# Layer 1 of a four-layer graph network: the last unit's norm, sides and scores in steps beside the first five jobs, with row 2 of the pairs among them, and the second head's values two pairs later

## The chip, the cores and the metric

The kernel is one program on one core of a Trainium2 chip. The metric is the device time of an execution in microseconds (us). The engines are named as in the profile: PE (matrix products and transposes, with weight loads as PEld), DVE (elementwise work and reductions), ACT (activation functions, copies), POOL (small elementwise work, some DMAs), SP (DMA issue). PE's clock can be lowered by a throttle; the profile shows the granted share.

## What is computed

Four layers on N = 4096 nodes of width D = 64 with one dense 0/1 adjacency matrix, each of the form x = x + layer(relu(layernorm(x))). Layer 0 is attention with eight heads and an output attention. Layer 1, around which the change lies, is a hyperbolic attention over all pairs of nodes:

```python
def _L1_gnn_ref(x, adj, r, w_att, b_att):
    c = 1.0 / r[0] ** 2
    x_t = logmap0(x, c)                       # x * artanh(sqrt(c)|x|) / (sqrt(c)|x|)
    left = x_t @ w_att[:D, 0]
    right = x_t @ w_att[D:, 0]
    adj_att = sigmoid(left[:, None] + right[None, :] + b_att[0]) * adj
    x_local = logmap(x[:, None, :], x[None, :, :], c)     # for every pair of nodes
    support_t = einsum('ij,ijd->id', adj_att, x_local)
    return proj(expmap(x, support_t, c), c)

h = maximum(layernorm(x), 0)
x = x + _L1_gnn_ref(h, adj, ...)
```

Layers 2 and 3 are a mean over neighbours with a dense layer, and a weighted sum over at most 100 neighbours.

## The kernel before

The nodes lie as NB = 32 blocks of P = 128, in NG = 8 groups of G = 512 (GB = 4 blocks each). The stages run one after the other: preparation, layer 0's heads, its output attention, a transition, layer 1's pairs, layer 1's nodes, layers 2 and 3.

**Layer 0's heads** run as 16 units (two halves of the targets, eight heads). A unit goes through the blocks in pairs j0 = 0, 2, 4 and so on; `split_edges` (L1229) makes the signs `st`, then B and C, and PE sums products with them (L1599). Beside the pairs of a unit the next head's values are prepared by a generator, `coming`, advanced by the condition at L1725: in the first unit two steps a pair from j0 = NB/2 + 4 = 20 on. Among these steps is an addition to FT (L1303) that waits for a DMA.

**Layer 0's output attention** runs as four units u of OB = 8 blocks (L2225 to L2329). A unit's results are finished (`finish_unit`, L2174: small folds on PE, DVE arithmetic, a tanh on ACT at L2217, the addition to x at L2222) beside the first products of the unit after it; then `layer1_nodes` (L1906) runs beside that unit: the norm of the new x (`norm_steps`, L994), h, its squared length a, the scale xs and its 16-bit pieces in the tile `aug`, the logarithms la and lb, and the sums with w_att (left, nrb). `layer1_sides` (L1994) transposes the pieces of `aug` into the four "sides" XC, LC, XH, LH that the products of pairs read, one PE transposition of eight blocks and one copy for each; `layer1_scores` (L2004) splits `left` into three 16-bit parts, transposes them and stores and reloads them by DMA as MOV.

**The transition** is what is left for the last unit, blocks 24 to 31 (L2331 to L2373). Its `finish_unit` runs with twelve side copies of the first three units spread through it; then come the rest of these, the last unit's `layer1_nodes` step by step, its four sides and its scores, and only then the pairs begin. A table load for the square root (L2355) comes before, one for the logarithm inside (L1931), one for the sigmoid after (L1948).

**The pairs** (`pairs_fast`, L2412) are 36 jobs (gi, gj) of two groups. The list `rows` sets their order: (0,0), (1,1), then rows 7, 6, 5, 4, 3, 2, each as (gi,0) to (gi,gi), at last (1,0). The loop runs over n = -2 to 36 and in each n over four slots s. In a slot the jobs are at different depths: for job n + 2 (`later`) `distance` (two products pu, L2480 and L2481, and an activation, L2482) and `square`; for job n + 1 (`soon`) `score_pair` (products pl, L2460 and L2466, sigmoid, L2471), `factor` and `weigh` on DVE; for job n (`now`) `turn` (transposes and a DVE product), `sums` and `last_column` (products accj and acci, L2526); for job n - 1 `bring`, which adds accj to VT on DVE (L2572, L2574). `check_edges` puts checks of the adjacency's rows (L972, one DVE pass of 1024 each) beside. A pair of different groups needs scores in both directions; one of a group with itself needs one, and no `turn`.

When the last job of rows 6, 4 and 2 has been brought, the two groups above it (a quarter of the nodes) are complete, and their `nodes` chain (`finish_steps`, L2644, then norm and two pieces of h, `hs` at L3233) is appended to `ends`; `end_nodes` takes steps from it in the slots of the following jobs, one chain after the other. The quarter of groups 0 and 1 comes after the last job. `scales()` sets the constants of these chains, once, at n = 3. While jobs follow, a chain takes its roots from `inverse_root` (L980: a first guess on DVE, then twelve small operations on POOL), not from ACT.

Order: inside `in_order()` (L933) the instructions of PE, DVE and ACT keep the order in which they are written; this holds for the transition and for the pairs. SP and POOL are free, apart from their data. A waiting instruction holds up all that is written behind it on its engine.

Of the kernel before, what the change touches and what calls it, by code (L numbers as in the profile page):

```python
# [25 lines left out]
P = 128  # L26
# [815 lines left out]
def kernel(  # L842
# [235 lines left out]
    with ExitStack() as l0:  # L1078
# [405 lines left out]
        with ExitStack() as ha:  # L1484
# [52 lines left out]
            for hf in range(2):  # L1537
# [9 lines left out]
                for hd in range(NH):  # L1547
# [85 lines left out]
                    for j0 in range(0, NB, 2):  # L1633
# [91 lines left out]
                        if j0 >= (NB // 2 + 4 if first else NB // 2 - 4):  # L1725
                            with behind(*done_at):
                                for _ in range(2 if first else 1):
                                    next(coming, None)
# [178 lines left out]
        def layer1_nodes(bs, work, aug, last=False):  # L1907
# [3 lines left out]
            yield from norm_steps(bs, work, "fat")  # L1911
# [17 lines left out]
            nc.scalar.activation(zn, zn, AF.Sqrt)  # L1929
            if last:  # L1930
                nc.scalar.preload_act_table_set("natural_log")  # L1931
# [5 lines left out]
            xh = aug[:, bs, C_XH : C_XH + D]  # L1937
# [3 lines left out]
            nc.vector.tensor_scalar(zn, zn, sqc, None, ALU.mult)  # L1941
            nc.vector.reciprocal(zr, zn)
            nc.vector.tensor_scalar(zn, zn, CLIP, None, ALU.min)
            nc.scalar.activation(la, zn, AF.Ln, bias=one_t, scale=1.0)
            nc.scalar.copy(aug[:, bs, C_XH2 : C_XH2 + D], xh)
            last_log[:] = [nc.scalar.activation(lb, zn, AF.Ln, bias=one_t, scale=-1.0).ins]
            if last:
                nc.scalar.preload_act_table_set("sigmoid_and_others")  # L1948
            nc.vector.tensor_tensor(aug[:, bs, C_XL : C_XL + D], t, xh, ALU.subtract)
# [7 lines left out]
            for i in range(2):  # L1957
                c = C_EX + 4 * i
                nc.vector.tensor_copy(
                    aug[:, bs, c : c + 4].rearrange("p b (k e) -> p b k e", e=2),  # L1960
# [4 lines left out]
                    aug[:, bs, c : c + 4].rearrange("p b (k e) -> p b k e", e=2),  # L1965
# [5 lines left out]
            nc.vector.tensor_copy(aug[:, bs, C_XH3 : C_XH3 + D], xh)  # L1971
            nc.vector.scalar_tensor_tensor(pab, pib, -1.0, pib, ALU.mult, ALU.max)
            yield False
            for i, dst in enumerate((left, nrb)):
                t = fat("hw")
                nc.vector.tensor_tensor(
                    t, hb, wab[:, i : i + 1, :].to_broadcast([P, n, D]), ALU.mult
                )
                nc.vector.tensor_reduce(dst[:, bs], t, AX.X, ALU.add)
                yield False  # L1980
# [12 lines left out]
        def layer1_sides(bs, bank, aug):  # L1993
            for b0 in range(bs.start, bs.stop, OB):  # L1994
                sides = (XC, C_XL, P), (LC, C_XH, P), (XH, C_XH2, KA), (LH, C_XH3, KA)
                for dst, c, cols in sides:
                    pt = bank()
                    for b in range(OB):
                        nc.tensor.transpose(
                            pt[:cols, b * P : (b + 1) * P], aug[:, b0 + b, c : c + cols], ident16  # L2000
# [3 lines left out]
        def layer1_scores(bs, ps):  # L2004
# [12 lines left out]
            pt = ps.tile([3 * n, P], F32, name="ppt", tag="misc")  # L2017
# [12 lines left out]
        wlast = el.enter_context(tc.tile_pool(name="wlast", bufs=2, side="right"))  # L2030
        with ExitStack() as ob:
# [193 lines left out]
            for u in range(4):  # L2225
# [8 lines left out]
                for q in range(NQ):  # L2234
# [62 lines left out]
                    if q == 0 and pending:  # L2297
                        finish_unit(*pending)
                        beside = layer1_nodes(slice((u - 1) * OB, u * OB), work, aug)
# [5 lines left out]
                if u == 3:  # L2305
                    layer1_scores(slice(0, NB - OB), ps)
# [31 lines left out]
            def bring(copy):  # L2338
                copy(*asked.pop(0))

            with in_order():
# [13 lines left out]
                nc.scalar.preload_act_table_set("sqrt_and_others")  # L2355
                ask(3)
                bring(nc.scalar.copy)
                chain = layer1_nodes(slice(NB - OB, NB), wlast, aug, True)
                for copy in (None, None, 1, 0, 1, 0, 0, None):
                    next(chain)  # L2360
                    ask()
                    if copy is not None:
                        bring(nc.vector.tensor_copy if copy else nc.scalar.copy)
                rest = layer1_sides(slice(NB - OB, NB), side, aug)
                for copy in (nc.scalar.copy, nc.vector.tensor_copy) * 2:
                    ask()
                    while asked:
                        bring(nc.vector.tensor_copy)
                    copy(*next(rest))
                assert next(coming, None) is None  # L2370
                for _ in chain:
                    pass
                layer1_scores(slice(NB - OB, NB), ps)  # L2373
# [3 lines left out]
    nc.vector.tensor_scalar(pm, pc, MIN_NORM, None, ALU.max)  # L2377
# [34 lines left out]
    def pairs_fast(es, VT, nodes, scales):  # L2412
# [4 lines left out]
        nc.vector.tensor_scalar(rb, nrb, -1.0, None, ALU.mult)  # L2417
# [10 lines left out]
        rows = [[(0, 0)], [(1, 1)]]  # L2428
        rows += [[(gi, gj) for gj in range(gi + 1)] for gi in reversed(range(2, NG))]
# [6 lines left out]
        with ExitStack() as ss:  # L2436
# [130 lines left out]

            def bring(gi, gj):
# [6 lines left out]
                if (gi, gj) in final:  # L2575
# [5 lines left out]
                    if gi % 2 == 0 and gi:  # L2581
                        bank = lambda: ps_f.tile([P, G], F32, name="pf", tag="pf")
                        ends.append([nodes(gi * GB, bank, beside), 0])
# [22 lines left out]
            load_edges(*jobs[0])  # L2606
            with in_order():
                for n in range(-2, len(jobs) + 1):
# [3 lines left out]
                    if n == 3:  # L2612
                        scales()
                    for s in range(4):
# [577 lines left out]
    with ExitStack() as es:  # L3192
# [10 lines left out]
        def scales():  # L3203
# [4 lines left out]
            )  # L3208
            nc.vector.tensor_scalar(pabs, pabs, sqc, 2.0 * F_C, ALU.mult, ALU.mult)
# [93 lines left out]
```

## Time and profile before

| | us |
|---|---|
| median of 3 runs | 1894.47 |
| lowest and highest | 1887.88, 1898.22 |
| the profiled execution, its own time | 1883.13 |
| its span | 1881.4 |

The stages in that trace: heads until about 905, output attention to 1109, transition to 1134, pairs to about 1595, the nodes' tail to about 1626, layers 2 and 3 to the end. The order of some pairs in it, by the end of the job's addition to VT: (1,1) starts its addition at 1167.31, (7,0) at 1181.61, (3,3) at 1546.17, (2,0) at 1559.88, (2,1) at 1571.43, (2,2) at 1579.59 and (1,0) at 1593.04.

The page's table of slices gives PE's granted clock in tenths of full speed, 40 slices of 47 us; the groups' rows give an instruction's busy time, its mean in ns, and the idle time ahead of it with what ended it:

```profile
PEclk8899999999999999999899997999999999999999
...
L2482 ACT ACTIVATE yt<-pu,consts 128x512 f32<-128x512 f32 x144 | 98.5, 686 | 95.8 <-PE pu L2481 95.8
...
L2471 ACT ACTIVATE sg<-pl,rb 128x512 f32<-128x512 f32 x256 | 160.6, 677 | 9.8 <-PE pl L2466 7.1
```

Slice 24, from 1129 to 1176, has one of the lowest clocks after the start of the program. Over the pairs ACT's idle time lies nearly all ahead of L2482, ended by PE: PE is the later of the two there.

### The profile page before, as it was taken

Reading aid. Unit: us, or ns where it says so; the run is one execution under the profiler, and the core shown is the slowest. Engines: PE = TensorE matmul, PEld = TensorE weight load, DVE = VectorE, ACT = ScalarE, POOL = GpSimd, SP = SyncE. Lnnn points to the kernel's source line nnn. Section 1 sums busy time; section 2 is a strip of 40 time slices with the busy share of each in tenths; the row PEclk is TensorE's granted clock in tenths of the full one; section 3 lists DMA queues with packets and bytes.
Section 4 is the critical chain, followed back from the end, with each engine's and each line's share of the span. In section 5 each row is a group of like instructions: output and inputs, shape, how many; then the busy total and the mean of one; then the engine's idle time right before and its main releaser. Section 6 shows DMA issues by size and latency. Waiting matters only on the chain.

```text
span 1881.4 us, 43986 instructions
## 1 busy us (share of the span) xinstructions
PE 1730.8 (92%) x19023; PEld 810.1 (43%) x19023; DVE 1606.5 (85%) x2480; ACT 1421.4 (76%) x1469; POOL 119.8 (6%) x204
## 2 busy tenths in 40 slices
PE   5789988999989999999899988999999998899998
PEld 4344444444445445445444442333333333464333
DVE  5889999999989989999778887998899787666787
ACT  2859988899978988899589978777777775234565
POOL 2001100010000000000121100000011022000000
PEclk8899999999999999999899997999999999999999
DMA  8966555535411110110455524454533111874595
GB/s 112 173 152 101 106 74 85 129 131 193 168 52 53 52 50 27 52 41 2 136 191 184 182 96 152 163 185 155 181 118 114 60 40 49 281 205 142 176 342 177
DMA packets 145996, 239.06 MB, mean 127 GB/s; under 512 B 16676, under 2 KB 106100, under 8 KB 140256
## 3 DMA queue, kind: packets, MB, share of 16 engines
q1 hardware_dynamic: 131264, 194.02, 31.4%
q0 software_dynamic: 14528, 42.13, 12.9%
q8 instruction: 151, 2.47, 0.5%
q14 instruction: 53, 0.43, 0.1%
HBM read 245.37 MB, written 49.46 MB: 157 GB/s over the span
## 4 chain that ended last, share of the span: by engine, by line
PE 48%; DVE 26%; ACT 15%; issue 7%; DMA 3%; POOL 0%; SPq 0%; DVEq 0%; ACTq 0%; POOLq 0%
ACT st L1242 9%; DVE B L1248 9%; PE accj L2526 9%; PE acco L2272 4%; PE accC L1599 4%; DVE st L1236 3%; PE pv L3105 3%; PE sacc L3129 3%; PE pf L2516 3%; PE pl L2460 2%; DVE C L1256 2%; PE pu L2480 2%; PE pl L2466 2%; PE accB L1599 2%; ACT sqy L2492 1%
## 5 line engine op out<-in xcount | busy, mean ns | idle before, releaser
L1242 ACT ACTIVATE st<-srow,nt 128x2048 int8<-128x2048 f32 x352 | 682.1, 1994 | 84.9 <-DVE B L1248 84.2
L1248 DVE TENSOR_TENSOR B<-st,mres 128x1024 int32<-128x1024 int32 x256 | 311.0, 1219 | 26.1 <-ACT st L1242 17.3
L1599 PE MATMUL accB<-B,ybh 128*32 128x512 fp8e4 x3072 | 255.8, 381 | 20.3 <-DVE B L1248 20.1
L1599 PEld LDWEIGHTS <-ybh 128*32 128x32 bf16 (+1 forms) x6656 | 180.7, 97 | 210.9 <-issue 55.2
L1599 PE MATMUL accD<-B,ybh 128*32 128x512 fp8e4 x2048 | 207.6, 382 | 2.3 <-DVE h L1747 2.3
L1236 DVE TENSOR_SCALAR st<-srow,nt 128x2048 uint8<-128x2048 f32 x160 | 205.0, 1283 | 1.5
L2526 PE MATMUL accj<-sg,who 128*64 128x512 f32 (+1 forms) x512 | 195.6, 611 | 5.6 <-DVE sg L2519 5.5
L2526 PE MATMUL acci<-sg,who 128*64 128x512 f32 (+1 forms) x512 | 195.6, 611 | 0.0
L1599 PE MATMUL accC<-mres,ych 128*32 128x512 fp8e4 x1920 | 190.0, 379 | 0.0
L1599 PE MATMUL accC<-B,ycn 128*32 128x512 fp8e4 x1920 | 190.0, 379 | 0.0
L2482 ACT ACTIVATE yt<-pu,consts 128x512 f32<-128x512 f32 x144 | 98.5, 686 | 95.8 <-PE pu L2481 95.8
L1256 DVE TENSOR_TENSOR C<-B,mres 128x1024 int32<-128x1024 int32 x136 | 166.2, 1222 | 4.6 <-PE accC L1599 1.7
L2471 ACT ACTIVATE sg<-pl,rb 128x512 f32<-128x512 f32 x256 | 160.6, 677 | 9.8 <-PE pl L2466 7.1
L1599 PEld LDWEIGHTS <-ych 128*32 128x32 f16 x4096 | 116.3, 97 | 119.2 <-issue 15.8
L1599 PE MATMUL accL<-B,ybh 128*32 128x512 fp8e4 x1536 | 156.4, 382 | 4.9 <-DVE h L1746 4.9
L1599 PE MATMUL accC<-C,ych 128*32 128x512 fp8e4 x2176 | 145.9, 383 | 9.0 <-DVE C L1256 8.9
L972 DVE SCALAR_TENSOR_TENSOR raw<-raw 128x1024 f32<-128x1024 f32 x128 | 153.9, 1215 | 0.0
L1242 ACT ACTIVATE st<-srowo,nto 128x1024 int8<-128x1024 f32 x128 | 138.1, 1136 | 13.4 <-DVE B L1248 10.5
L3119 ACT ACTIVATE w3b<-pv 128x512 int16<-128x512 f32 x172 | 91.0, 597 | 55.7 <-ACT w3b L3119 23.2
L2460 PE MATMUL pl<-nm,noid 128*128 128x512 fp8e4 x256 | 82.0, 387 | 15.5 <-ACT sg L2471 15.3
L2500 DVE SCALAR_TENSOR_TENSOR yt<-sqy,yt 128x1024 f32<-128x1024 f32 x72 | 84.8, 1217 | 0.7 <-ACT sqy L2492 0.7
L2507 DVE SCALAR_TENSOR_TENSOR sg<-yt,sg 128x1024 f32<-128x1024 f32 x72 | 84.8, 1217 | 0.5 <-ACT sg L2471 0.5
(544 smaller groups left out, 2666.1 us busy)
## 6 DMA issues: line engine op xcount, KB each, us to landing
raw<-in_adj_dram SPq DMA_DIRECT2D x128, 512.0 KB, 4.4
mo<-edges SPq DMA_DIRECT2D x32, 512.0 KB, 3.9
noedge<-nmo POOLq DMA_DIRECT2D x32, 512.0 KB, 3.6
nm<-noedge SPq DMA_DIRECT2D x64, 256.0 KB, 3.0
m<-edges SPq DMA_DIRECT2D x32, 512.0 KB, 5.8
srow<-srow_d SPq DMA_DIRECT2D x15, 1024.0 KB, 9.1
mres<-in_adj_dram POOLq DMA_DIRECT2D x8, 1024.0 KB, 36.1
edges<-in_adj_dram POOLq DMA_DIRECT2D x8, 1024.0 KB, 14.9
```

Source lines behind the costliest of these rows:

```text
L972: nc.vector.scalar_tensor_tensor(raw, raw, 0.0, raw, ALU.is_gt, ALU.not_equal, accum_out=bad[:, c : c + 1])
L1236: nc.vector.tensor_scalar(st[:, i, :].bitcast(U8), srow, negs[:, i : i + 1], EDGE, ALU.is_gt, ALU.mult)
L1242: nc.scalar.activation(st[:, i, :], srow, AF.Sign, bias=negs[:, i : i + 1], scale=-1.0)
L1248: nc.vector.tensor_tensor(B.bitcast(I32), st.bitcast(I32), edges.bitcast(I32), ALU.bitwise_and)
L1256: nc.vector.tensor_tensor(C.bitcast(I32), B.bitcast(I32), edges.bitcast(I32), ALU.bitwise_xor)
L1599: ins = nc.tensor.matmul(acc[k * O : (k + 1) * O, :], lhsT=values, rhs=moving(k), start=start, stop=stop,)
L2460: nc.tensor.matmul(pl, lhsT=noid, rhs=nm[:, b, :].bitcast(F8), start=True, stop=False)
L2471: nc.scalar.activation(sg[:, b0 + k, :], pl, AF.Sigmoid, bias=rb[:, j : j + 1], scale=1.0)
L2482: nc.scalar.activation(far[gi, gj][:, b, :], pu, AF.Sigmoid, bias=nb_t, scale=2.0 * DIST_K / (DIST_S * DIST_S),)
L2500: nc.vector.scalar_tensor_tensor(y, squares.pop((gi, gj, b0)), F_K1, y, ALU.add, ALU.mult)
L2526: nc.tensor.matmul(acc[r : r + n, :], lhsT=XQ[:, src, cols], rhs=w, start=start, stop=stop)
L3119: nc.scalar.activation(wk, pvs[i, k], AF.Relu)
```

## The change

- The last unit's work leaves the transition and becomes a generator, `last_unit`, of twenty steps: one is taken in each slot of the jobs n = -2 to 2. In n = -2 and -1 it does the norm, in n = 0 the scale and the pieces in `aug`, in n = 0 (last slot) to 1 the sides, in n = 1 the logarithms, then left, nrb and in n = 2 the scores. Its PSUM tiles come from the pool of `turn`.
- For this unit both roots are taken by `inverse_root`; the table of the logarithm is loaded for `logs()`, and the sigmoid's back, in n = 1. The pieces go to a tile of their own, `aug_last`. All four side copies are DVE's. `rb` (the bias of the sigmoid) is set in two parts, and `pm` in `scales()`.
- The seven side copies of the other units that are left after `finish_unit` go alternately to ACT and DVE.
- Row 2 comes right behind (1,1), not ahead of (1,0), so that five jobs, (0,0) to (2,2), go before row 7. The chains of quarters are appended after the last jobs of rows 6, 4 and 3 (row 2 before), and take two steps in each slot but the first of row 3's jobs (2, 1 and 2 before, in rows 3 and 2). In (1,0) they take up to four a slot, before and after.
- The four row checks of n = -1 go, those of the slots begin at n = 3.
- The second head's values start at pair j0 = 24, not 20.

```diff
-                        if j0 >= (NB // 2 + 4 if first else NB // 2 - 4):
+                        if j0 >= (NB - 8 if first else NB // 2 - 4):
...
-            yield from norm_steps(bs, work, "fat")
+            yield from norm_steps(bs, work, "fat", beside=(last,))
...
             nc.vector.tensor_scalar(zn, ab, MIN_NORM, None, ALU.max)
-            nc.scalar.activation(zn, zn, AF.Sqrt)
             if last:
-                nc.scalar.preload_act_table_set("natural_log")
+                root = inverse_root("zn_root", zn, work)
+                nc.gpsimd.tensor_tensor(zn, zn, root, ALU.mult)
+            else:
+                nc.scalar.activation(zn, zn, AF.Sqrt)
...
+            xh = aug[:, :, C_XH : C_XH + D]
             nc.scalar.copy(xh, t)
             yield False
 
-            nc.vector.tensor_scalar(zn, zn, sqc, None, ALU.mult)
-            nc.vector.reciprocal(zr, zn)
-            nc.vector.tensor_scalar(zn, zn, CLIP, None, ALU.min)
-            nc.scalar.activation(la, zn, AF.Ln, bias=one_t, scale=1.0)
-            nc.scalar.copy(aug[:, bs, C_XH2 : C_XH2 + D], xh)
-            last_log[:] = [nc.scalar.activation(lb, zn, AF.Ln, bias=one_t, scale=-1.0).ins]
-            if last:
-                nc.scalar.preload_act_table_set("sigmoid_and_others")
-            nc.vector.tensor_tensor(aug[:, bs, C_XL : C_XL + D], t, xh, ALU.subtract)
+            def logs():
+                nc.vector.tensor_scalar(zn, zn, sqc, None, ALU.mult)
+                nc.vector.reciprocal(zr, zn)
+                nc.vector.tensor_scalar(zn, zn, CLIP, None, ALU.min)
+                nc.scalar.activation(la, zn, AF.Ln, bias=one_t, scale=1.0)
+                last_log[:] = [nc.scalar.activation(lb, zn, AF.Ln, bias=one_t, scale=-1.0).ins]
+
+            if not last:
+                logs()
+            nc.scalar.copy(aug[:, :, C_XH2 : C_XH2 + D], xh)
+            nc.vector.tensor_tensor(aug[:, :, C_XL : C_XL + D], t, xh, ALU.subtract)
...
             yield False
+            if last:
+                logs()
+                yield True
             for i, dst in enumerate((left, nrb)):
...
                     pt = bank()
                     for b in range(OB):
                         nc.tensor.transpose(
-                            pt[:cols, b * P : (b + 1) * P], aug[:, b0 + b, c : c + cols], ident16
+                            pt[:cols, b * P : (b + 1) * P],
+                            aug[:, b0 - bs.start + b, c : c + cols],
+                            ident16,
                         )
...
-        def layer1_scores(bs, ps):
...
-            pt = ps.tile([3 * n, P], F32, name="ppt", tag="misc")
+            pt = bank()[0 : 3 * n, 0:P]
...
+        aug_last = wlast.tile([P, OB, C_EL + KX], F16, name="aug_last", tag="aug", bufs=1)
...
-                        beside = layer1_nodes(slice((u - 1) * OB, u * OB), work, aug)
+                        us1 = slice((u - 1) * OB, u * OB)
+                        beside = layer1_nodes(us1, work, aug[:, us1])
...
-                    layer1_scores(slice(0, NB - OB), ps)
+                    layer1_scores(
+                        slice(0, NB - OB), lambda: ps.tile([P, G], F32, name="ppt", tag="misc")
+                    )
...
                 finish_unit(*pending, beside_unit)
-                nc.scalar.preload_act_table_set("sqrt_and_others")
-                ask(3)
-                bring(nc.scalar.copy)
-                chain = layer1_nodes(slice(NB - OB, NB), wlast, aug, True)
-                for copy in (None, None, 1, 0, 1, 0, 0, None):
-                    next(chain)
-                    ask()
-                    if copy is not None:
-                        bring(nc.vector.tensor_copy if copy else nc.scalar.copy)
-                rest = layer1_sides(slice(NB - OB, NB), side, aug)
-                for copy in (nc.scalar.copy, nc.vector.tensor_copy) * 2:
-                    ask()
-                    while asked:
-                        bring(nc.vector.tensor_copy)
-                    copy(*next(rest))
-                assert next(coming, None) is None
-                for _ in chain:
-                    pass
-                layer1_scores(slice(NB - OB, NB), ps)
-
-
-
-    nc.vector.tensor_scalar(pm, pc, MIN_NORM, None, ALU.max)
+                for k in range(7):
+                    ask(2)
+                    bring(nc.vector.tensor_copy if k % 2 else nc.scalar.copy)
+                assert not asked and next(coming, None) is None
+
+        def last_unit(bank, rb):
+
+            bs = slice(NB - OB, NB)
+            chain = layer1_nodes(bs, wlast, aug_last, True)
+            for _ in range(10):
+                yield next(chain)
+            sides = layer1_sides(bs, lambda: bank().bitcast(F16), aug_last)
+            for side in sides:
+                yield True
+                nc.vector.tensor_copy(*side)
+            yield from chain
+            layer1_scores(bs, bank)
+            yield True
+            nc.vector.tensor_scalar(rb[:, bs], nrb[:, bs], -1.0, None, ALU.mult)
...
-        nc.vector.tensor_scalar(rb, nrb, -1.0, None, ALU.mult)
+        seen_b = slice(0, NB - OB)
+        nc.vector.tensor_scalar(rb[:, seen_b], nrb[:, seen_b], -1.0, None, ALU.mult)
...
-        rows = [[(0, 0)], [(1, 1)]]
-        rows += [[(gi, gj) for gj in range(gi + 1)] for gi in reversed(range(2, NG))]
+        rows = [[(0, 0)], [(1, 1)], [(2, gj) for gj in range(3)]]
+        rows += [[(gi, gj) for gj in range(gi + 1)] for gi in reversed(range(3, NG))]
         rows.append([(1, 0)])
...
+            def bank():
+                return ps_f.tile([P, G], F32, name="pf", tag="pf")
...
-                    if gi % 2 == 0 and gi:
-                        bank = lambda: ps_f.tile([P, G], F32, name="pf", tag="pf")
-                        ends.append([nodes(gi * GB, bank, beside), 0])
+                    if gi in (3, 4, 6):
+                        ends.append([nodes(gi // 2 * 2 * GB, bank, beside), 0])
...
+            unit = last_unit(bank, rb)
             with in_order():
...
                     if n == 3:
+                        assert next(unit, None) is None
                         scales()
...
                         if now:
-                            end_nodes(s, 4 if not soon else 1 + s % 2 * (now[0] < 4) if s else 0)
+                            end_nodes(s, 4 if not soon else 1 + (2 < n and now[0] < 4) if s else 0)
+                        next(unit, None)
                         if s == 1 and soon:
                             factor(*soon)
-                        if n > 1 and soon and s % 2 == 0:
+                        if n > 2 and soon and s % 2 == 0:
                             check_edges(1 if busy else 2 if s or now[0] == now[1] else 1)
                         if s == 3 and soon:
                             weigh(*soon)
-                            check_edges(4 if n < 0 else 0)
...
+            nc.vector.tensor_scalar(pm, pc, MIN_NORM, None, ALU.max)
```

More of the change, by code (lines that the diff above doesn't have):

```diff
@@ L1936, in layer1_nodes @@
             nc.vector.tensor_tensor(t, hb, over(ps2, D), ALU.mult)
-            xh = aug[:, bs, C_XH : C_XH + D]
+            xh = aug[:, :, C_XH : C_XH + D]
             nc.scalar.copy(xh, t)
             yield False
-            nc.vector.tensor_scalar(zn, zn, sqc, None, ALU.mult)
-            nc.vector.reciprocal(zr, zn)
-            nc.vector.tensor_scalar(zn, zn, CLIP, None, ALU.min)
-            nc.scalar.activation(la, zn, AF.Ln, bias=one_t, scale=1.0)
-            nc.scalar.copy(aug[:, bs, C_XH2 : C_XH2 + D], xh)
-            last_log[:] = [nc.scalar.activation(lb, zn, AF.Ln, bias=one_t, scale=-1.0).ins]
-            if last:
-                nc.scalar.preload_act_table_set("sigmoid_and_others")
-            nc.vector.tensor_tensor(aug[:, bs, C_XL : C_XL + D], t, xh, ALU.subtract)
+            def logs():
[8 more added lines that the diff above has]
+            nc.vector.tensor_tensor(aug[:, :, C_XL : C_XL + D], t, xh, ALU.subtract)
             ef = work.tile([P, 2, n], F32, name="ef", tag="ef", bufs=1)
@@ L1959, in layer1_nodes @@
                 nc.vector.tensor_copy(
-                    aug[:, bs, c : c + 4].rearrange("p b (k e) -> p b k e", e=2),
+                    aug[:, :, c : c + 4].rearrange("p b (k e) -> p b k e", e=2),
                     e16[:, :, i].unsqueeze(2).to_broadcast([P, n, 2, 2]),
@@ L1964, in layer1_nodes @@
                 nc.vector.tensor_scalar(
-                    aug[:, bs, c : c + 4].rearrange("p b (k e) -> p b k e", e=2),
+                    aug[:, :, c : c + 4].rearrange("p b (k e) -> p b k e", e=2),
                     e16[:, :, 1 - i].unsqueeze(3).to_broadcast([P, n, 2, 2]),
@@ L1970, in layer1_nodes @@
                 )
-            nc.vector.tensor_copy(aug[:, bs, C_XH3 : C_XH3 + D], xh)
+            nc.vector.tensor_copy(aug[:, :, C_XH3 : C_XH3 + D], xh)
             nc.vector.scalar_tensor_tensor(pab, pib, -1.0, pib, ALU.mult, ALU.max)
             yield False
+            if last:
+                logs()
+                yield True
             for i, dst in enumerate((left, nrb)):
@@ L1999, in layer1_sides, with layer1_scores @@
                         nc.tensor.transpose(
-                            pt[:cols, b * P : (b + 1) * P], aug[:, b0 + b, c : c + cols], ident16
+                            pt[:cols, b * P : (b + 1) * P],
+                            aug[:, b0 - bs.start + b, c : c + cols],
+                            ident16,
                         )
                     yield dst[:, b0 * P : (b0 + OB) * P], pt[:cols]
-        def layer1_scores(bs, ps):
+        def layer1_scores(bs, bank):
             n = bs.stop - bs.start
```

## The prediction

> **What bounds the kernel now.** I read the page's busy shares first, then the table of windows around the place that the change cuts open, then the timeline there and at the end of the pairs.
>
> ```profile
> PE 1730.8 (92%) x19023; PEld 810.1 (43%) x19023; DVE 1606.5 (85%) x2480; ACT 1421.4 (76%) x1469; POOL 119.8 (6%) x204
> ```
>
> PE is nearly full over the whole, so time can only be won where PE is not. Windows (width, then busy us of PE, PE's weight loads, DVE, ACT, POOL, each with its count; then PE's granted clock, DMA share, GB/s):
>
> ```profile
> 1115.00:1120.00 5.00, 4.61 (x67) 4.51 (x65) 3.34 (x9) 2.96 (x4) 0.00 (x0) 1.00 0.00 0
> 1120.00:1125.00 5.00, 0.61 (x8) 0.45 (x7) 4.29 (x8) 4.14 (x7) 0.00 (x0) 0.99 0.00 0
> 1125.00:1130.00 5.00, 0.81 (x8) 0.82 (x9) 4.29 (x21) 4.76 (x9) 0.00 (x0) 0.50 0.00 0
> 1130.00:1135.00 5.00, 4.22 (x31) 3.12 (x29) 3.01 (x7) 2.89 (x4) 0.59 (x3) 0.50 0.09 29
> 1135.00:1140.00 5.00, 4.67 (x12) 1.05 (x10) 4.22 (x14) 4.89 (x7) 0.00 (x0) 0.50 0.96 273
> ...
> 1150.00:1155.00 5.00, 5.00 (x18) 0.98 (x14) 4.31 (x4) 3.50 (x6) 0.00 (x0) 0.78 0.94 311
> 1155.00:1160.00 5.00, 4.21 (x23) 0.98 (x22) 3.61 (x5) 4.66 (x7) 0.00 (x0) 1.00 0.11 33
> ```
>
> From 1120 to 1130 PE works 1.4 us of 10, its clock halves, and it stays halved until about 1152. This hole is what the change attacks: the last unit's norm and sides stand alone there, DVE and ACT passing single operations to each other. The timeline names its edges (start, us, instruction, in brackets the idle time before it and its releaser):
>
> ```profile
> 1118.33 0.42 ACT L2217 ACTIVATE nmo<-nmo 128x256 f32<-128x256 f32 x1 [1.36 <-DVE nmo L2216]
> 1118.77 1.28 ACT L2355 ACT_TABLE_LOAD   x1
> ...
> 1129.19 3.60 PE L1999 MATMUL trd<-ident,aug 128*128 128x128 f16 x32 [7.46 <-DVE aug L1959]
> 1133.57 0.61 PE L2480 MATMUL pu<-XAf,LDf 128*128 128x512 f16 x1 [0.78 <-DVE LDf L2369]
> ...
> 1593.04 0.64 DVE L2574 TENSOR_TENSOR VT<-VT,accj 128x512 f32<-128x512 f32 x1
> ...
> 1625.02 0.69 DVE L3233 SCALAR_TENSOR_TENSOR hs<-h,XAf 128x512 f32<-128x512 f32 x1 [0.70 <-ACT XAf L3230]
> 1629.85 0.48 PE L2840 MATMUL pm<-wsq,ones 64*128 64x64 f32 x2 [4.98 <-DVE wsq L2838]
> ```
>
> The last tanh ends at 1118.75, the first product of pairs starts at 1133.57: 14.8 us. The other edge is the end: after the last pair's add (1593.04) the nodes' chain runs on DVE to 1625.71, 32.7 us later, and PE then waits 4.98 us for constants queued behind it. From 1200 to 1400 PE is 97% busy and DVE 83 to 90%: there nothing is to be had, and little may be added.
>
> **The change part by part**, against the profiled execution (1883.13 us; its span 1881.4).
>
> *Values two pairs later.* No operation is added or removed. DVE is 91 to 97% busy in the 100-us windows of that stage, and its sum of work is what ends it. The one wait that could move, 2.92 us before the add of FT at 116.19 for a DMA, keeps its place in DVE's order. Behind it the 14th pair's B and C change places with value steps, which PE's products wait for; SP's store of values now goes ahead of a row load. Ends: -2 (the whole wait goes, nearly) to +1 (one DVE operation of 1.22 us exposed). I take **-0.5**.
>
> *The start of the pairs.* After the last tanh seven copies of sides remain, four on ACT at 1.01 us: first pair product at 1118.8 + 4.1 = 1122.9 rather than 1133.57, so **-10.7** at that point. Then the last unit has to be paid beside jobs. The first jobs' score work is ACT's: its rows (1.25 per two sigmoids or tanh, 1.15 a square) sum to 4.6, 7.1, 7.1 and 9.6 us for the four slots before pair (1,1) is added, 28.4 us; before it took from 1134.8 to 1167.3, 32.5. ACT gets in addition ln_sq, hh and two casts (0.63, 0.63, 0.62, 0.61), two logarithms (0.60) and two table loads, for the logarithms and back to the sigmoid (2 x 1.28): 5.6 us. Three table loads go (L2355, L1931, L1948), but out of the stretch already counted. Floor: 28.4 + 5.6 = 34.0, so (1,1) done by about 1156.8, **-10.5**.
>
> It will not keep that floor. Both roots move to POOL, twelve operations each. The nearest row is the nodes' root later in the stage (1393.11 to 1398.96, the first three at 1.03 to 1.06 us, the rest 0.20): 5.9 us each. ACT and DVE run in written order, so DVE's h waits for POOL with this slot's weigh behind it, and ACT's Square of h and cast of xs wait for DVE with the slot's sigmoids and squares behind them. I estimate 2.9 us of ACT stall for xs and 1.7 for smaller waits: 38.6 us, (1,1) at 1122.9 + 0.7 + 38.6 = 1162.2, **-5.1**.
>
> Here a rule speaks for the change and the row against it. The Trainium skill, page "TensorE: Matmul & The Clock Gate", section "What's actually happening", gives full clock after about 3.4 us of sustained work, half after an idle window as long. In these slots PE has 1.8, 3.5, 5.5 and 7.2 us of work at full clock, 46% of 39 us, in gaps under 3.4 us: by the rule the clock stays up, and -5.1 stands. The trace is harsher: the clock fell at 1350 and 1428 after 2-us stretches with PE at 23 to 38%, and came back in the windows above only after 18.5 us with PE 84 to 100% busy, when a stretch from 1148.0 to 1152.1 had no gap. So the row says: it falls, as before, soon after 1123. Then PE's 18 us become 36, matching ACT, and their alternation costs an estimated 3.6: (1,1) at 1165.8. I take the row: **-1.5**. Ends: -10.5 (no stall, full clock) and +3 (each wait doubled).
>
> *Row 2 right behind.* Slot n = 2 (pair (2,0)) now has the head of a row, two sums of hw, scores and a transpose: DVE about 14.5 us, so 15 to 16 against the 14.3 that (7,0) took there (1167.31 to 1181.61). With (2,1) at 12 and (2,2) at 11, the row costs about 38.7 at the front. At the end it took 1546.17 to 1579.59, 33.4, and (3,3), 10.5 there, becomes last but one and should take (2,2)'s 8.2: saving 35.7; (7,0) behind a diagonal pair gets 0.6 shorter. Row 2 was cheap at the end because no row checks were left for DVE (last at 1481). Net +2.4 to +4.5, taken **+3.0**.
>
> *Checks.* Four left the idle DVE at n = -1, but by row 7 seven are done rather than four; the total is the same. Their cover is PE. 0.
>
> *Nodes.* Quarter 4,5 had rows 3 and 2 to run beside; now row 3 alone, two steps in each of three slots, and (1,0), four a slot as before. DVE has room, PE is the bound there: 0 to +2, taken +0.5. Quarter 2,3, started behind (2,2) before, now queues behind quarter 4,5 in (1,0)'s slots. In the order on DVE some 13 of its operations (the sum xu to the reciprocal of un, with two ACT round trips) that stood ahead of the last add stand behind it, with the three constants from ident. By their rows (0.69 x 4, 0.17 to 0.23 x 9, constants 0.87, waits about 0.7) that is **+6.1** behind the last add; the last job gets an estimated 1.4 shorter, as these no longer delay its add. PE does not hide it: it waits 4.98 us already for the end of this chain. +4.7 by the sum; PE's work of layer 2 may be reordered a little into the gap, I take **+4.0**. Ends +2 and +6.5; a longer gap may also keep the clock (0.66 in the window 1630 to 1635) low longer, 0 to +2.
>
> *Sum:* -0.5 - 1.5 + 3.0 + 0.5 + 4.0 = **+5.5 us**. That makes 1883.13 + 5.5 = 1888.6 by the profiled execution, which stands 11.3 below the median of the runs shown; carried to the median, 1894.47 + 5.5 = **1900.0**. About 0.5% (9.5 us) is what a measurement of this kernel can tell from no change, so the forecast is *no difference to be told*, on the slow side.
>
> **The rivals.**
>
> *A. The slow clock lasts through the first full pair: slower.* Place: pair (2,0). Off-diagonal pairs need 12.9 us of PE at full clock; with the half clock throughout, PE alone takes 25. For it: the clock stayed at 0.50 for 27 us before, and the new start has more and smaller gaps spread over a longer stretch; the return needs four gapless microseconds, which PE fed in turn with ACT does not easily get. Against it: at half clock slot n = 1 has 14.4 us of PE work beside ACT's 13.4, which closes the gaps, as at 1148. Price 8 us if it returns in the last third of (2,0); it decides from about 4 us on, since 5.5 + 4 is the bound of what can be told. Time: 1894.5 + 13.5 = **1908**.
>
> *B. The start is all gain and the end is covered: faster.* ACT finds its inputs ready, the clock holds as the rule has it: -10.5; row 2 costs at the front what it did at the end, 12.9 + 11 + 11 = 35 against 35.7; and layer 2's products of the quarters ready first fill PE while quarter 2,3 is late: 0. With -0.5 for the values: about -11, **1884**. For it: PE is 95 to 100% busy from 1600 to 1625 with such products. Against: two in-order engines behind POOL chains of 5.9 us, and the wait of 4.98 that shows the end exposed.
>
> *C. The edits move work but nothing that ends last*: gain of the start and losses of row 2 and the end cancel, 1894.5. In the orders on the engines all twenty steps do go beside the jobs, so the change does what it says; this case differs from the forecast in sizes alone, and its chance is in the forecast's.
>
> **How the numbers follow.** Forecast (with C) 0.48, A 0.35, B 0.17. The forecast's bounds spill 0.01 to A's side: faster 0.17, same 0.47, slower 0.36. The bounds of the costs, taken all at their ends, give -10.8 to +16; not all fall together, so the forecast's own range is 1892 to 1905. To leave out no more than two in ten it reaches to both rivals: 1884 to 1911.
>
> **What would show it.** Each step by itself:
> - the first pu (L2480) right behind the last tanh's copies, near 1123; the add of (1,1) near 1166 (right), near 1157 (B);
> - granted clock in the windows from 1120: half until 1150 to 1165; 1.00 throughout speaks for the rule and B; half beyond 1170 for A;
> - ACT idle ahead of the cast of xs, released by DVE, and DVE idle ahead of h, released by POOL;
> - (2,0) at 15 to 16 us between adds; row 2 at about 38.7;
> - from the last add to the last hs (L3233) 38.8 us in place of 32.7, and the wait before pm (L2840) near 9 us in place of 4.98;
> - layer 0's heads ending within 2 us of before.
>
> The prediction is wrong if the start gains more than 5 us, or if the last hs is not later behind the last add.

## The result, and the profile after

| | before | changed |
|---|---|---|
| median of 20 runs, us | 1889.84 | 1899.3 |
| lowest, highest | 1881.89, 1898.51 | 1892.04, 1907.69 |
| span of the profiled execution | 1881.4 | 1899.4 |

The ratio is 1.0049 (95%: 1.0034 to 1.0063), about 9.3 us slower. The two profiled executions differ by 18.0 us, twice that, so I read them by stages, from the last tanh of the transition (T) on. "(1,1)" in the table is the start of its addition to VT; the times of pairs given ahead of the prediction are starts too. What a pair "took" is the time from the start of the addition before it to the start of its own. The long rows of pairs repeat to a tenth of a us from trace to trace; but T itself is spread over 1118.1 to 1123.1 in the fourteen traces of this case, and the time from pm to the end over 251.2 to 259.0, with both orders of pairs in both ends of that spread. Before's profiled execution was at the short end of both.

| us | before | changed | difference | predicted |
|---|---|---|---|---|
| T | 1118.75 | 1121.10 | +2.35 | -0.5 |
| T to first product of pairs | 14.82 | 3.68 | -11.14 | -10.7 |
| T to (1,1) | 48.56 | 48.48 | -0.1 | -1.5 |
| (1,1) to last add | 425.73 | 433.77 | +8.0 | +2.1 |
| last add to pm | 36.81 | 41.64 | +4.8 | +5.4 |
| pm to the end | 251.6 | 254.4 | +2.8 | 0 to +2 |

The prediction's +4.0 for the end is divided here as it was worked out: +6.1 behind the last add, less 0.7 that layer 2's products were to hide, and -1.4 in the last job, ahead of that add. So its +2.1 is 3.0 + 0.5 - 1.4.

The first row of the changed kernel's page shows nearly the same shares as before, with 13.3 us more on PE, whose clock was low for longer (0.965 on average, before 0.973):

```profile
PE 1744.1 (92%) x19008; PEld 812.6 (43%) x19023; DVE 1608.7 (85%) x2484; ACT 1418.1 (75%) x1465; POOL 123.7 (7%) x217
```

Windows of it over its new start (columns as before: PE, PE's loads, DVE, ACT, POOL; granted clock; DMA):

```profile
1120.00:1125.00 5.00, 2.79 (x46) 2.50 (x44) 4.75 (x12) 4.05 (x5) 0.74 (x3) 1.00 0.15 44
1125.00:1130.00 5.00, 4.53 (x14) 1.35 (x13) 0.78 (x2) 4.40 (x7) 0.00 (x0) 0.62 0.94 285
1130.00:1135.00 5.00, 4.02 (x10) 0.80 (x9) 2.44 (x3) 4.37 (x7) 3.17 (x7) 0.50 0.90 338
1135.00:1140.00 5.00, 3.67 (x9) 0.89 (x9) 1.58 (x3) 4.93 (x8) 1.21 (x6) 0.50 0.05 16
1140.00:1145.00 5.00, 4.30 (x12) 0.72 (x10) 4.21 (x11) 2.18 (x5) 2.03 (x6) 0.67 0.18 52
1145.00:1150.00 5.00, 2.27 (x12) 1.07 (x12) 4.66 (x14) 3.23 (x5) 3.34 (x8) 0.67 0.01 3
```

The hole of ten microseconds is gone: PE works in every window. But it is not full in any of these, its clock halves as before, and between 1140 and 1150 ACT too is idle for 4.6 us. After a return at 1143.3 the clock fell three times more before row 7, once like this, with no gap on PE longer than 2.13 us in the ten us ahead of it:

```profile
1163.80:1167.21 3.41, 1.08 (x6) 0.20 (x4) 1.68 (x2) 3.38 (x6) 0.00 (x0) 1.00 0.22 65
1167.21:1170.62 3.41, 3.41 (x16) 1.36 (x15) 0.94 (x2) 2.42 (x4) 0.00 (x0) 0.50 0.00 0
```

The timeline names what they wait for (start, us, instruction; idle before it and releaser), and below the two waits the new end:

```profile
1124.78 0.38 PE L2493 MATMUL pu<-XAf,LDf 128*128 128x512 f16 x1 [2.12 <-ACT LDf L2352]
...
1143.62 0.62 ACT L1940 CAST aug_last<-xs 128x512 f16<-128x512 f32 x1 [2.82 <-DVE xs L1938]
...
1147.73 1.03 PE L2006 MATMUL pf<-ident,aug_last 128*128 128x128 f16 x8 [3.43 <-ACT aug_last L1952]
...
1181.08 0.37 PE L2027 MATMUL pf<-ident,parts 128*24 128x128 f32 x1 [2.75 <-DVE parts L2025]
...
1588.95 0.68 DVE L2590 TENSOR_TENSOR VT<-VT,accj 128x512 f32<-128x512 f32 x1
...
1603.35 0.68 DVE L2590 TENSOR_TENSOR VT<-VT,accj 128x512 f32<-128x512 f32 x1
...
1640.16 0.69 DVE L3251 SCALAR_TENSOR_TENSOR hs<-h,XAf 128x512 f32<-128x512 f32 x1 [0.69 <-ACT XAf L3248]
1644.99 0.66 PE L2857 MATMUL pm<-wsq,ones 64*128 64x64 f32 x2 [6.88 <-DVE wsq L2855]
```

Three waits of the last unit stand in the jobs, at 1143.62, 1147.73 and 1181.08, each 2.8 to 3.4 us: the 11 us won at the first product are spent by (1,1), and the third falls into (2,0), which takes 18.2 us:

```profile
1169.58 0.69 DVE L2588 COPY VT<-accj 128x512 f32<-128x512 f32 x1 [4.10 <-PE acci L2539]
...
1187.78 0.69 DVE L2590 TENSOR_TENSOR VT<-VT,accj 128x512 f32<-128x512 f32 x1 [1.87 <-PE accj L2539]
```

The addition at 1588.95 is (3,3)'s; it waited for nothing, so DVE itself was late. The last hs ends 37.5 us behind the last add (before 32.7), and PE's wait ahead of pm has grown from 4.98 to 6.88.

### The profile page after: what moved, and what is told of

It is laid out like the page before. It is cut to its first block, busy times and chain, and to the rows that moved or that the text cites. A ratio compares the mean times of both kernels' runs of the same rounds, so it can differ in the third digit from the quotient of the medians.

```text
span 1899.4 us, 43987 instructions
## 1 busy us (share of the span) xinstructions
PE 1744.1 (92%) x19008; PEld 812.6 (43%) x19023; DVE 1608.7 (85%) x2484; ACT 1418.1 (75%) x1465; POOL 123.7 (7%) x217
## 3 DMA queue, kind: packets, MB, share of 16 engines
q0 software_dynamic: 14528, 42.13, 12.8%
## 5 line engine op out<-in xcount | busy, mean ns | idle before, releaser
L2539 PE MATMUL accj<-sg,who 128*64 128x512 f32 (+1 forms) x512 | 199.8, 622 | 9.3 <-DVE sg L2532 9.1
L2539 PE MATMUL acci<-sg,who 128*64 128x512 f32 (+1 forms) x512 | 199.8, 622 | 0.0
L1242 ACT ACTIVATE st<-srowo,nto 128x1024 int8<-128x1024 f32 x128 | 137.9, 1137 | 14.2 <-DVE B L1248 11.3
```

The costliest lines, as they stand in the source:

```text
L1242: nc.scalar.activation(st[:, i, :], srow, AF.Sign, bias=negs[:, i : i + 1], scale=-1.0)
L2539: nc.tensor.matmul(acc[r : r + n, :], lhsT=XQ[:, src, cols], rhs=w, start=start, stop=stop)
```

## Experiments

All stage times are from the traces, in us; "T to pm" is 511.1 in the kernel before and 523.9 in the changed one.

**The values alone** (kernel before, one edit).

```diff
-                        if j0 >= (NB // 2 + 4 if first else NB // 2 - 4):
+                        if j0 >= (NB - 8 if first else NB // 2 - 4):
```

> The kernel before with one edit of the change: the second head's values start at pair 24. Theory A (the loss lies in the order of pairs and at their end): no difference, -2 to +1 us, layer 0's heads end within 1 us of before's 902 us. Theory B (the values are a cause, since in the first pair of traces the heads ended 1.7 us later although they began 2.4 us earlier): +3 to +5 us, heads end 2 to 4 us later after their first product.

Ratio 1.0003 (0.9986 to 1.0021), the last products of layer 0's heads start at 900.96 (before 901.08), T 1119.74, T to pm 509.6. No effect; theory B, which rested on one pair of traces, falls.

**The order alone** (kernel before: row 2 in front, the chains behind rows 6, 4, 3 and their steps; the last unit still in the transition).

```diff
-        rows = [[(0, 0)], [(1, 1)]]
+        rows = [[(0, 0)], [(1, 1)], [(2, gj) for gj in range(3)]]
...
-                    if gi % 2 == 0 and gi:
+                    if gi in (3, 4, 6):
...
-                            end_nodes(s, 4 if not soon else 1 + s % 2 * (now[0] < 4) if s else 0)
+                            end_nodes(s, 4 if not soon else 1 + (2 < n and now[0] < 4) if s else 0)
```

> The kernel before with row 2 behind (1,1), the chains of quarters behind rows 6, 4 and 3 and their steps as in the change; the last unit stays in the transition. Theory A: most of the loss is here: (2,0) takes 14.3 us as (7,0) did, row 2 about 36.5 at the front against 32.5 saved behind (3,3), the last hs 37 us behind the last add instead of 32.7: +8 us together. Theory C (the steps of the last unit beside the pairs are the cause): +2 us or less.

Ratio 1.0076 (1.0049 to 1.0103). T to (1,1) 50.65, row 2 14.3 + 11.0 + 12.0 = 37.3, (1,1) to last add 430.9, T to pm 523.1; from the last add to pm 4.75 more than before. Its end, on DVE and PE:

```profile
1603.92 0.68 DVE L2574 TENSOR_TENSOR VT<-VT,accj 128x512 f32<-128x512 f32 x1
...
1640.65 0.69 DVE L3233 SCALAR_TENSOR_TENSOR hs<-h,XAf 128x512 f32<-128x512 f32 x1 [0.70 <-ACT XAf L3230]
1645.48 0.66 PE L2840 MATMUL pm<-wsq,ones 64*128 64x64 f32 x2 [6.75 <-DVE wsq L2838]
```

37.4 us from the last add to the end of the last hs, with the last unit where it always was: theory A. The order alone costs 5.1 from (1,1) to the last add and 4.75 after it. The row in front isn't dear: 37.3, less than the 38.7 of the prediction. It is the end that gives back too little: from (4,4) to the last add 65.2 here and 65.3 in the changed kernel, 97.3 before, so 32.1 are saved. The 2.1 us ahead of (1,1) I leave open: that stretch took 47.0 to 48.6 in the three traces with the old transition and the old order, one of them with products added in the transition, and 50.65 in this one.

**Three node steps in a slot of row 3** (changed kernel).

```diff
-    end_nodes(s, 4 if not soon else 1 + (2 < n and now[0] < 4) if s else 0)
+    end_nodes(s, 4 if not soon else 1 + 2 * (2 < n and now[0] < 4) if s else 0)
```

> The changed kernel, with three node steps in a slot of row 3 instead of two, so that quarter 4,5 is done before (1,0) and quarter 2,3 has (1,0)'s slots. Theory A (the end is exposed): last add to last hs falls from 37.5 to 33 to 34 us, the wait before pm to about 5 us, row 3 not more than 1 us longer: -3 to -4 us against the changed kernel, ratio to before about 1.003. Rival: DVE becomes the bound in row 3, which gets longer by what the end gains: no difference.

Row 3 took 53.3 rather than 50.8, (1,0) 12.7 rather than 14.4, last add to last hs 35.6 rather than 37.5; ratio to before 1.0072 (1.0038 to 1.0106). From (4,4) to the last hs that is 101.6 against 102.7: the rival, but for 1.1 us. DVE is the bound in row 3, and most of what the end gains row 3 loses. Ahead of that (2,0) took 19.8 in this trace, with the changed kernel's own code there; the next run says more of it.

**Scores three slots later** (changed kernel).

```diff
             yield from chain
+            for _ in range(3):
+                yield True
             layer1_scores(bs, bank)
...
```

> The changed kernel, with the last unit's scores three slots later, in job (2,1) instead of (2,0). Theory A (in (2,0) PE, which works in written order, waits 2.75 us for the small DVE chain ahead of the scores' transposition, and its clock falls to 0.66 behind it): (2,0) 18.2 us becomes 14.5 to 15.5, (2,1) 11.2 becomes 11.5 to 12.5: -2 to -3 us. Rival: the wait moves along with the transposition: (2,0) and (2,1) together stay at 29.4 us.

(2,0) 14.0, (2,1) 13.1, (2,2) 9.9: 37.0 for the row against 40.1, 3.0 us less from (1,1) to the last add, as theory A has it. Changed kernel first, this one second, same window:

```profile
1180.00:1185.00 5.00, 3.92 (x13) 1.06 (x13) 4.24 (x16) 1.27 (x2) 0.00 (x0) 0.66 0.19 56
```

```profile
1180.00:1185.00 5.00, 5.00 (x32) 2.09 (x33) 4.90 (x16) 4.19 (x6) 0.00 (x0) 1.00 0.02 5
```

ACT goes from 1.27 busy to 4.19: one waiting transposition of 0.37 us on PE had held up the products written behind it, and ACT with them. The whole time (1.0073, 1.0045 to 1.0101) doesn't resolve 3 us.

Not all of the 3.0 is the wait. Three more kernels (below: the clock held, the roots on DVE, and node steps as before) have the scores where the changed kernel has them, and took 16.7 in (2,0) and 38.6 in the row. In the last of these the transposition waits as long, and the clock stays at 1.00 behind it:

```profile
1178.33 0.27 PE L2027 MATMUL pf<-ident,parts 128*24 128x128 f32 x1 [2.75 <-DVE parts L2025]
```

```profile
1175.00:1180.00 5.00, 2.25 (x15) 0.74 (x13) 4.31 (x15) 1.63 (x4) 0.00 (x0) 1.00 0.01 1
1180.00:1185.00 5.00, 5.00 (x31) 1.92 (x28) 4.39 (x16) 3.64 (x6) 0.00 (x0) 1.00 0.19 55
```

In the changed kernel the clock fell behind the wait (0.66 in the window above), in the run with three node steps for longer (0.59 from 1180 to 1185, 0.73 to 1190). So (2,0) took 16.7 with the clock kept behind the wait, 18.2 and 19.8 without. (With the roots on DVE the clock was low ahead of the wait, which was 1.91 us there, and (2,0) took 16.7 too.) About half of the 3.0, 1.6 us, is the row's gain over 38.6; the rest goes along with that fall of the clock, which came in two of the five traces with the scores there.

**Clock held at the start** (changed kernel with products that nothing reads: 16 of 256 columns behind the last transposition of the sides, and four of 512 in each of ten slots).

```diff
+            for _ in range(times):
+                nc.tensor.matmul(pt[:, 0:w], lhsT=ident16, rhs=rhs, start=True, stop=True)
...
+                        if n < 0 or n == 0 and s < 2:
+                            hold(held, XC[:, 0:G], 4)
...
```

> The changed kernel with products added that nothing reads: 16 behind the last transposition of sides, four of 512 columns in each slot from n = -2 to the second of n = 0, to hold PE's clock at full through the start. Clock theory: clock 1.00 from 1120 to 1165, and the time from the last tanh to the add of (1,1) falls from 48.5 by the 3.6 us that the prediction put on the halved clock, or more. Rival (ACT and the waits for DVE and POOL set the start): the clock holds and the start stays within 1 us of 48.5, or is longer by the added work.

T to (1,1) 48.8. Its windows:

```profile
1125.00:1130.00 5.00, 4.63 (x23) 2.04 (x21) 0.95 (x3) 2.81 (x4) 0.63 (x3) 1.00 0.60 167
1130.00:1135.00 5.00, 4.88 (x24) 1.78 (x22) 1.36 (x3) 4.76 (x9) 0.62 (x2) 1.00 0.95 303
1135.00:1140.00 5.00, 5.00 (x24) 2.06 (x23) 2.09 (x3) 4.93 (x7) 3.74 (x12) 1.00 0.59 216
...
1145.00:1150.00 5.00, 0.32 (x6) 0.32 (x7) 4.21 (x14) 4.39 (x7) 4.18 (x10) 1.00 0.01 2
1150.00:1155.00 5.00, 5.00 (x28) 1.75 (x29) 3.39 (x4) 1.92 (x3) 0.78 (x2) 0.66 0.00 0
```

The clock was 1.00 from 1120 to 1150, and the start was not shorter: ACT still waited 2.81 us for xs, and PE, at full clock, stood almost still from 1145 to 1150, until the pieces of aug came:

```profile
1145.58 0.62 ACT L1940 CAST aug_last<-xs 128x512 f16<-128x512 f32 x1 [2.81 <-DVE xs L1938]
```

```profile
1149.68 0.51 PE L2006 MATMUL pf<-ident,aug_last 128*128 128x128 f16 x6 [4.69 <-ACT aug_last L1952]
```

ACT's waits from T to (1,1) sum to 9.7 us in both kernels. The rival holds, within a bound: the added products cost time themselves (the first product of pairs came at T + 4.54 rather than 3.68, and ACT waited 0.49 for the second pair of them), so by an estimate from these up to 1.4 us may be the halved clock's, not 3.6. The same start with the clock falling 4.6 us later (node steps as before) took 47.6.

**The roots on DVE** (changed kernel; the operations of `inverse_root` issued on `nc.vector` for the last unit).

```diff
-                root = inverse_root("zn_root", zn, work)
+                root = inverse_root("zn_root", zn, work, nc.vector)
...
```

> The changed kernel with the last unit's two roots on DVE in place of POOL. Theory (POOL's latency reaches ACT through DVE): h follows the second root step without the 2.9 us wait, xs comes earlier, ACT's 2.8 us wait for xs is gone or under 1 us, tanh to (1,1) falls from 48.5 to about 45.5. Rival: 24 more operations on DVE (0.17 each, 4.1 us) make weigh and factor late instead: no difference at (1,1).

T to (1,1) 50.8, longer by 2.3; ACT's wait for xs grew from 2.82 to 5.45:

```profile
1148.23 0.62 ACT L1942 CAST aug_last<-xs 128x512 f16<-128x512 f32 x1 [5.45 <-DVE xs L1940]
```

h did come 1.9 us earlier after T (13.7 in place of 15.6), but nothing came of it: the reduction behind it, which needs ACT's square of h, started at T + 18.0 in both kernels. And the second root's operations, 2.6 us of them, now stand ahead of xs in DVE's order, where POOL had worked beside. Worse even than the rival: POOL was the right engine.

**Five pairs of a group with itself in front** (changed kernel, chains and their steps as before the change; with the roots on DVE as well in a second run).

```diff
-        rows = [[(0, 0)], [(1, 1)], [(2, gj) for gj in range(3)]]
+        rows = [[(gi, gi)] for gi in range(5)]
+        rows += [[(gi, gj) for gj in range(gi + (gi > 4))] for gi in reversed(range(1, NG))]
...
```

> The changed kernel with the five jobs beside the last unit all pairs of a group with itself, (0,0) to (4,4), row 2's other two back at the end before (1,0), chains and their steps as before the change. Theory (row 2 in front costs PE time and bares the end): PE has room beside these jobs, so no wait of the last unit falls on a full PE; (4,4) added about 76 us after the tanh, last add at 463 to 470 us after it (changed kernel 482.3, before 474.3), last hs 32.7 behind it: 5 to 11 us faster than before, ratio 0.994 to 0.997. Rival (a pair of a group with itself hides in a row only because the pair ahead fills PE; five in a row pay for ACT and for bringing): last add at 476 or later, no gain on before.

> The same with the roots on DVE. If POOL's latency is what delays the start there too, 2 to 3 us faster than the diagonals alone; otherwise the same.

T to (1,1) 44.3, the start that gained most: 4.3 us. But the other pairs took 15.6, 11.3 and 14.0 in front, and rows 4, 3, 2 got only 9.1 to 9.3 shorter each without theirs than before; last add at T + 479.5, the last hs 35.5 behind it and not the expected 32.7, T to pm 519.2, ratio 1.0038 (1.0023 to 1.0054). With the roots on DVE (1,1) comes at T + 46.3, T to pm is 524.2, ratio 1.0072 (1.0047 to 1.0097): slower, not 2 to 3 us faster. The rival: what such a pair saves in a row is less than it costs beside the last unit.

**Products that nothing reads in the hole of the kernel before** (56 of them ahead of the last unit's sides).

```diff
+                hold(held, aug[:, 0, 0 : 4 * D], 56)
                 rest = layer1_sides(slice(NB - OB, NB), side, aug)
```

> The kernel before, with 56 products of 256 columns that nothing reads ahead of the last unit's sides, to fill PE's 7.5 us hole in the transition. It measures what the halved clock costs before. Clock theory (as the prediction had it): clock 1.00 from 1120 to 1150, and tanh to the add of (1,1) falls from 47 to 51 (three traces) to 44 to 45. Rival (ACT sets it, as in the changed kernel with the clock held): 46 to 48, no more than the spread.

Clock 1.00 until 1135, half from about 1138 to 1155; T to (1,1) 47.6, inside the spread; ratio 0.9987 (0.9969 to 1.0005). As the rival has it. The clock fell again inside the pairs, so this run does not hold it where it was meant to, and it doesn't settle what the halved clock costs before. It seems to cost something there: the values alone, with the same code from T on, had the clock back at T + 28.6, before's trace at T + 33.4, and took 47.0 against 48.6 to (1,1).

**Node steps as before** (changed kernel; 2, 1, 2 in the slots of row 3).

```diff
-    end_nodes(s, 4 if not soon else 1 + (2 < n and now[0] < 4) if s else 0)
+    end_nodes(s, 4 if not soon else 1 + s % 2 * (2 < n and now[0] < 4) if s else 0)
```

> The changed kernel with 2, 1 and 2 node steps in the slots of row 3, as before the change. If row 3 and (3,3), 11.0 us where 8.2 was foreseen, are longer because DVE carries quarter 4,5's chain there, row 3 gets 1 to 2 us shorter and the last hs comes as much or more later behind the last add (37.5 to 39 or 40): no gain. If DVE has room, row 3 stays at 50.8.

Row 3 took 15.8 + 12.7 + 11.4 + 9.1 = 49.0, 1.8 less, and the last hs came 37.3 behind the last add, not later. Its additions for (3,2) and (3,3):

```profile
1573.86 0.68 DVE L2590 TENSOR_TENSOR VT<-VT,accj 128x512 f32<-128x512 f32 x1
...
1582.98 0.68 DVE L2590 TENSOR_TENSOR VT<-VT,accj 128x512 f32<-128x512 f32 x1
```

9.1 us between them, still without a wait: one step fewer in a slot shortens a job that DVE bounds. Ratio 1.0057 (1.0041 to 1.0074): the whole time doesn't show the 1.8.

**xs ahead of the slot's weigh, and the scores late** (changed kernel).

```diff
-            for _ in range(10):
-                yield next(chain)
+            for k in range(10):
+                step = next(chain)
+                yield next(chain) if k == 7 else step
...
```

> The changed kernel with the scores late as in the fourth run, and xs taken on DVE ahead of the weigh (2.35 us) of its slot, the cast a slot later as it was. If the written order on DVE is what ACT waits for (2.8 us at the cast of xs, with clock held and with DVE roots still there): that wait falls under 1 us and tanh to (1,1) from 48.5 to about 46; tanh to the wait before pm from 523.9 to about 518. Rival: PE's wait for the pieces of aug grows by the same, (1,1) stays at 48.5.

T to (1,1) 49.0. The waits of ACT and of PE in that stretch:

```profile
1138.71 0.62 ACT L1942 CAST aug_last<-xs 128x512 f16<-128x512 f32 x1 [0.67 <-DVE xs L1938]
1142.85 0.69 ACT L2500 ACTIVATE yt<-pu,consts 128x512 f32<-128x512 f32 x1 [2.35 <-PE pu L2499]
```

```profile
1139.87 1.11 PE L2544 MATMUL accj<-sg,who 128*64 128x512 f32 x1 [1.23 <-DVE sg L2525]
1145.28 0.93 PE L2008 MATMUL pf<-ident,aug_last 128*128 128x128 f16 x7 [1.62 <-ACT aug_last L1954]
```

The wait for xs fell to 0.67 as foreseen, and another took its place: the weigh comes later, PE's sums wait 1.23 us for it, and ACT behind PE 2.35. The rival's result, by another way than it named: PE's wait for the pieces of aug fell from 3.43 to 1.62. T to pm 521.3, not the expected 518, ratio 1.0049 (1.0031 to 1.0067).

**Both repairs** (scores late, node steps as before).

> The changed kernel with both repairs that gained by themselves: scores three slots later (3.0 us in row 2) and 2, 1, 2 node steps in row 3 (1.8 us there). If the two are separate terms of the sum, row 2 takes 37.0 and row 3 49.0, tanh to the wait before pm 523.9 falls to 518.5 to 519.5, and what is left against before (511.1) is the order of rows and the end: ratio to before about 1.004. If they share a cause, 520.5 or more.

Row 3 49.0 as foreseen, row 2 39.1 and not 37.0: in (2,0) and (2,2) the clock was lower (0.53 and 0.78 from 1165 to 1175, 0.79 and 0.87 from 1200 to 1210, where the scores late alone had 0.66 and then 1.00). T to pm 520.6, ratio 1.004 (1.0021 to 1.0058). By the bound set for it, 520.5, the sum failed. Job by job row 3 added as foreseen and row 2 did not; the 2.1 us that are missing go along with the clock, but no run held it there. No version of the changed kernel beats the kernel before.

## Why the prediction was right, and where it was off

The forecast was 5.5 us slower; 9.3 were measured (6.4 to 11.9 by the interval). The direction and the reason of its sum hold: a start that gains nearly nothing, and an order that costs time, with a longer end. The size was 0.6 of the measured one, and "no difference to be told" was too careful: the interval leaves out zero. That the median 1899.3 lies beside the forecast 1900.0 is luck: the forecast started from 1894.47, and the kernel before measured 1889.84 beside the change. Step by step:

- **Values later**, -0.5: no effect found, as said; the range of -2 to +1 stands.
- **First product**, -10.7: -11.1.
- **(1,1)**, -1.5: -0.1, right in size for a reason that was half wrong. Of the prediction's 8.2 us of stall, 4.6 were waits and 3.6 the halved clock. The wait for xs was foreseen at 2.9 and took 2.82. The clock did fall, and again at 1167.21, where PE's longest gap in ten us had been 2.13 us, so before's row was right on this, against the rule of the Trainium skill that the prediction weighed (page "TensorE: Matmul & The Clock Gate", section "What's actually happening": half clock after an idle window of about 3.4 us). But held at full it gained an estimated 1.4 at most. What stands in its place is a second wait in written order that the prediction didn't have at this size: 3.43 us of PE for the pieces of aug, and behind it 3.42 of ACT. And the order on DVE, not POOL's latency, stands behind the first: xs waited behind a weigh of 2.35 us. (The floor of 1156.8 also leaves out the 0.7 that the next sum adds.)
- **Row 2 in front**, **nodes** and the last job, +2.1: together +8.0. This is the step that was mis-sized. The row itself was not: 38.7 foreseen, 40.1 in the changed kernel's trace, 38.6 in three others and 43.3 in the one where the clock was low longest; (2,0) was longer than said (16.7 and more, for 15 to 16, with the transposition on PE that waits for the end of DVE's small chain) and (2,1) and, but for that one, (2,2) shorter. What failed is the saving at the end: 32.1 in place of 36.6 (35.7, and 1.4 in the last job, less 0.5 for the nodes). (3,3) was to take (2,2)'s 8.2 as the last but one, but took 11.0, as DVE carries quarter 4,5's chain there; (1,0) was to get 1.4 shorter and got about 1 longer. "DVE has room, PE is the bound there" was wrong for row 3: three steps made it 2.5 longer, one fewer 1.8 shorter. By kernels, the order alone measured +5.1, and the last unit beside the jobs adds 2.9 in the changed kernel's trace, about 1.6 in the runs with the clock held and with the roots on DVE.
- **The end**, +5.4: +4.8 with the last unit in steps and 4.75 with it in the transition, so the moved operations are its cause. Behind the last add they came to 1.3 less than the 6.1 of their rows; that +4.7 stands in the prediction's sum too is chance, as it holds the 1.4 that never came.
- **After pm**, 0 to +2: nothing that can be told from the spread of 251.2 to 259.0; a kernel with the new end had 251.3.
- **The bounds**, -10.8 to +16: the ends given for the parts sum to -8.1 and +19.
- **Rival A**, the clock low through (2,0), 8 us: not so; a second fall there cost about 1.5. The "four gapless microseconds" were too much: in the changed kernel full clock came back at 1143.3, with no gap on PE since 1139.70. **Rival B**, a start without stalls and a covered end: neither.

The stages sum to 12.8 from T to pm, 0.9 more than the top of the measured interval. 1.5 of it is likely the fall of the clock in (2,0) in that one trace; the rest stays open, as only profiled executions have stages.

## What to carry to other kernels

Where engines keep the written order, moving an idle stretch's work beside busy jobs pays only as far as its instructions don't wait at their places in it: here a chain of small DVE operations ahead of one transposition of 0.37 us stopped PE for 2.75 us and ACT with it, and taking one wait away let the next appear. So move the consumer some slots behind its producer first, and count the time to the end of the stage, not the first product. And what makes the new work fit, here another order of jobs, has a price of its own: try it alone before the rest is built on it; it was 10 of 12.8 us. Jobs that were to give time back have to be read for the engine that bounds them: row 3 lost to DVE what the sum had taken from PE. And a difference of 1.5 us between single traces can be the clock: compare several kernels with the same code at that place.

## What was not expected of the hardware

Holding PE's clock at 1.00 with 56 added products (16 of 256 and 40 of 512 columns) over a stretch that had run at 0.5 to 0.67 did not shorten it (48.8 against 48.5): there PE waited anyway. In (2,0), behind PE's wait, the clock's fall goes along with 1.5 and 3.1 us more (18.2 and 19.8 against 16.7). Moving the 24 operations of two roots from POOL (most 0.20 us, four of 1.06 to 1.13) to DVE (0.17 each) made the start 2.3 us longer, because POOL's time was beside DVE's.
